# Four graph layers on one core: batches exchanged inside the row tiles, row mixing on 64x64 blocks, rows loaded four groups ahead

## The chip, the cores and the metric

The kernel runs on 1 core of one Trainium2 chip. Time is device time of one execution in microseconds (us); lower is better. A core has five instruction queues that run beside one another: TensorE (PE, matrix products; its weight loads are shown as PEld), VectorE (DVE), ScalarE (ACT), GpSimd (POOL) and SyncE (SP, which here only issues DMAs). All data are f32.

## The reference, cut to what matters

There are 128 batches of 64 nodes with 256 features, and one 64x64 matrix `adj` that all layers share. Four layers follow one another, each with a residual and a layer norm.

```python
w = adj * adj                                       # layer 0: three graph convolutions
h = relu(w @ (x @ W1)); h = relu(w @ (h @ W2))
x = layernorm(x + w @ (h @ W3))
# layer 1: U = eigenvectors of the normalized Laplacian of adj
x = layernorm(x + U @ (relu((U.T @ x) @ W1 + b1) @ W2 + b2))
# layer 2: two graph convolutions (Wg0, Wg1), then for p = 1..4 an LSTM over windows of p nodes;
#          its last hidden state replaces node p-1 of each window
x = layernorm(x + h)
# layer 3: attention among the 64 nodes of a batch, masked by adj
x = layernorm(x + softmax(mask(h @ h.T)) @ h + b)   # h = x @ W + b_lin
```

## The kernel before, in words

The 8192 rows (128 batches x 64 nodes) are cut into 16 groups of 8 batches. A group is a tile of 128 partitions, 4 columns of rows and 256 features: column t holds two batches, one in partitions 0 to 63 and one in 64 to 127. Four groups live in `X` and twelve in `XA`; `order` is the sequence in which layer 0 takes them (groups 4 to 15, then 0 to 3).

**Phase A** is `layer0`, one loop over the groups. `burst` (its matmuls are L1068) mixes by `w` and transposes in one step: 32 matmuls of 64x64 blocks, one for each of the four corners of the array in turn. The three weight products are done by Strassen's seven products each (`seven`, with `by_first`, `by_second`, `by_third`; their matmuls all have line L977). The last convolution's mixing is `mix_rows`: before the change two calls per group, each one matmul of the full 128x128 block-diagonal `sqT2` over 512 moving columns (also L977; in the profile `ps<-s,sqT`, two PE instructions for one f32 matmul), then a DVE addition to the rows and the pieces of the layer norm. `bank` hands out PSUM banks in turn: 3 with the tag `ps`, 2 `ch`, 2 `b5`. `step` holds back a product's PSUM reader until the next product is issued and pops one piece of a norm.

Beside the matmuls runs `eigen`, the eigenvectors of the Laplacian: a long chain of tiny DVE steps (L52 with the other DVE work of this phase, its PE steps L312). It is a generator that `between` advances by a counted clock `now`, so its instructions stand between those of the products at fixed places. PE, DVE, ACT and POOL run in the order of the program text here (`manual_schedule`). SP, and the ten lines after `layer0` (L1235 to L1244: row sums of `adj`, halved and summed biases, written as `rs_row`, `adH2`, `rs_col`, `wide["c_b0"]`, `cbi`, `dbb`), were outside of this and were put by a scheduler: it set five of those DVE instructions among the first 51 us.

All input DMAs but three go through SP, in this order: a group, `aw1`, `aw2`, a group, `aw3`, the other 14 groups (L921), the constants of `eigen` (L924), and then the weights and biases of later layers (L890 to L959). After them SP issues `sh<-sh` and `sh<-h` (L1174, L1175) for each group, copies that `by_third` needs, and `rest<-XA`, the finished rows of a group.

**Phase B** is layers 1 to 3, all with line L162: `unit` records the operations of two groups at a time in a `Plan`, which simulates them with written costs and emits them engine by engine, up to four units in flight. `left_over` is what was left of phase A's norm pieces. The last two groups (`ENDING`, 14 and 15) take a shorter way through `from_lstm` and `layer3`: transposes on PE, attention in two halves of a group, norms whose scaling is on ACT (`scalar=True`, with `nm`, the negative mean times `rs`). `long` is the LSTM for p = 3 and 4 on two groups at once, `fast` one step of it; the last step's result is written in the order node, batch.

## Time and profile before

| what | value |
|---|---|
| median of 3 runs | 2268.37 us (2267.16 to 2269.09) |
| the profiled execution's own time | 2269.74 us, span 2267.9 us, mean granted TensorE clock 0.995 |
| PE, DVE, ACT, POOL busy | 2222.0, 1758.5, 1241.2, 207.9 us |
| phase A, start to the last `mix_rows` | 0 to about 821 us |
| phase B | about 821 us to the end |
| DMA | 163.05 MB, 264 GB/s in the first 57 us, 72 GB/s in the mean |

The profile is one execution. "busy" is time in which an engine had an instruction; the idle time before an instruction is put down to what it waited for ("<-"). The timeline gives start and duration of merged runs of like instructions. For PE the starts are what to read: a duration contains the way through the array, and the next matmul starts before it is over. One f32 matmul is two PE instructions. The view by stretches gives, for each stretch of the span, its length and the busy time and number of instructions of PE, PEld, DVE, ACT and POOL, then the granted clock, the busy share of the DMA engines (as the view reckons it) and GB/s.

### The profile page before, as it was taken

The numbers are of one execution on the slowest core, as the hardware profiler recorded it, in microseconds if no ns is written. First come the engines' busy times: TensorE is split into PE (matmuls) and PEld (weight loads), VectorE is DVE, ScalarE is ACT, GpSimd is POOL, SyncE is SP. The second block draws the span as 40 slices with busy tenths as digits, with TensorE's granted clock in tenths as the row PEclk, the third lists the DMA queues.
The fourth block names the chain that finished last, engine by engine and source line by source line (L and its number), as shares of the span: only waits on it lengthen the run. The fifth ranks groups of instructions, "written<-read, shape, count | busy, mean of one in ns | idle before, by whom it ended". The sixth has DMA issues, their size and how long they took to land.

```text
span 2267.9 us, 53164 instructions
## 1 busy us (share of the span) xinstructions
PE 2222.0 (98%) x20840; PEld 2026.8 (89%) x20840; DVE 1758.5 (78%) x5925; ACT 1241.2 (55%) x2999; POOL 207.9 (9%) x390
## 2 busy tenths in 40 slices
PE   7999999999999999999999999999999999999996
PEld 5998888888888878999999999999999999999985
DVE  5888888878888759765967977977977877578977
ACT  3455555545554445665655655655655655566554
POOL 0111111111111110000100000000000010000112
PEclk9999999999999999999999999999999999999998
DMA  8443333344332240000211211211211211002331
GB/s 264 96 92 77 85 75 85 87 91 94 85 85 66 66 155 29 20 1 20 76 38 41 78 66 50 78 57 50 87 57 41 84 65 35 31 29 65 109 113 54
DMA packets 95243, 163.05 MB, mean 72 GB/s; under 512 B 24976, under 2 KB 65936, under 8 KB 94992
## 3 DMA queue, kind: packets, MB, share of 16 engines
q1 hardware_dynamic: 83840, 120.05, 15.8%
q0 software_dynamic: 10800, 39.33, 9.2%
q8 instruction: 164, 2.69, 0.5%
q14 instruction: 87, 0.71, 0.1%
q10 hardware_dynamic: 352, 0.28, 0.0%
HBM read 57.64 MB, written 45.09 MB: 45 GB/s over the span
## 4 chain that ended last, share of the span: by engine, by line
PE 89%; DVE 6%; DMA 2%; ACT 1%; issue 1%; SPq 1%; POOL 1%; ACTq 0%; POOLq 0%; DVEq 0%
PE ps L162 59%; PE ch L977 15%; PE b L977 7%; PE ps L977 6%; PE ps L1068 2%; DVE w L162 1%; PE pa L312 1%; DVE D L52 1%; DMA XA<-in_x_dram 1%; DVE gates L162 1%; DVE X L162 1%; ACT gates L162 0%; DVE h L52 0%; DVE tw L52 0%; SPq L921 0%
## 5 line engine op out<-in xcount | busy, mean ns | idle before, releaser
L162 PE MATMUL ps<-w,wih 128*128 128x128 f32 (+2 forms) x2944 | 572.8, 298 | 2.1 <-DVE gates L162 0.9
L162 PEld LDWEIGHTS ps<-w,wih 128*128 128x128 f32 x2944 | 453.8, 191 | 28.5 <-issue 6.2
L162 PE MATMUL ps<-w,sums 128*128 128x128 f32 (+2 forms) x3104 | 476.6, 293 | 0.0
L162 PEld LDWEIGHTS ps<-w,sums 128*128 128x128 f32 x3104 | 423.5, 191 | 14.1 <-issue 1.9
L162 ACT ACTIVATE gates<-gates,cbi 128x256 f32<-128x256 f32 (+4 forms) x736 | 314.0, 479 | 174.0 <-DVE gates L162 172.0
L162 DVE TENSOR_TENSOR gates<-gates,ps 128x512 f32<-128x512 f32 (+4 forms) x408 | 234.2, 585 | 173.1 <-PE ps L162 159.7
L162 ACT COPY gates<-ps 128x512 f32<-128x512 f32 (+4 forms) x408 | 203.8, 505 | 253.8 <-PE ps L162 247.8
L986 ACT ACTIVATE h<-h 128x512 f32<-128x512 f32 x141 | 88.8, 629 | 283.3 <-DVE h L52 283.2
L162 PE MATMUL ps<-hs,whh 128*128 128x128 f32 (+1 forms) x896 | 181.2, 284 | 0.1
L162 PE MATMUL ps<-w,whh 128*128 128x128 f32 (+1 forms) x896 | 181.1, 284 | 0.0
L162 POOL TENSOR_SCALAR rs<-mv 128x2 f32<-128x2 f32 x96 | 27.5, 297 | 1318.5 <-DVE mv L162 1317.0
L162 ACT ACTIVATE gates<-ps,cbi 128x128 f32<-128x128 f32 (+2 forms) x368 | 119.1, 383 | 43.4 <-PE ps L162 43.1
L162 PEld LDWEIGHTS ps<-hs,whh 128*128 128x128 f32 x896 | 139.7, 191 | 0.3 <-DVE hs L162 0.3
L162 PEld LDWEIGHTS ps<-w,whh 128*128 128x128 f32 x896 | 139.7, 191 | 0.0
L977 PE MATMUL ch<-m,tw 128*128 128x256 f32 x512 | 120.6, 380 | 3.5 <-DVE h L52 3.5
L977 PE MATMUL b<-ss,aw 128*128 128x256 f32 x512 | 122.6, 379 | 0.0
L977 PEld LDWEIGHTS ch<-m,tw 128*128 128x128 f32 x512 | 96.2, 190 | 17.2 <-DVE h L52 4.7
L977 PEld LDWEIGHTS b<-ss,aw 128*128 128x128 f32 x512 | 96.3, 190 | 12.7
L1060 POOL DMA_DIRECT2D sh<-h x60 | 53.2, 957 | 485.9 <-PE b L977 148.8
L162 ACT ACTIVATE gates<-c 128x256 f32<-128x256 f32 (+1 forms) x176 | 75.5, 433 | 27.9 <-DVE c L162 26.2
L162 PE MATMUL ps<-hs,sums 128*128 128x128 f32 (+1 forms) x448 | 90.6, 284 | 0.0
L162 DVE TENSOR_TENSOR w<-w,w 128x128 f32<-128x128 f32 (+2 forms) x264 | 80.5, 316 | 8.9 <-PE ps L162 4.4
(384 smaller groups left out, 4281.2 us busy)
## 6 DMA issues: line engine op xcount, KB each, us to landing
sh<-h POOLq DMA_DIRECT2D x60, 512.0 KB, 5.8
far<-w SPq DMA_DIRECT2D x42, 512.0 KB, 2.8
w<-far SPq DMA_DIRECT2D x168, 128.0 KB, 3.1
X<-rest SPq DMA_DIRECT2D x24, 512.0 KB, 3.4
out_dram<-X SPq DMA_DIRECT2D x64, 128.0 KB, 1.8
sh<-sh SPq DMA_DIRECT2D x15, 512.0 KB, 2.9
sh<-h SPq DMA_DIRECT2D x15, 512.0 KB, 2.9
sh<-sh POOLq DMA_DIRECT2D x15, 512.0 KB, 4.6
```

The costliest lines, as they stand in the source:

```text
L52: return getattr(self.engine, name)(out, *args, **kw)
L162: getattr(e, name)(*[real(x) for x in args], **{k: real(v) for k, v in kw.items()})
L312: PE.matmul(out, lhsT, rhs, start=True, stop=True)
L977: PE.matmul(out, lhsT, rhs, start=start, stop=stop, **kw)
L986: S.activation(dst, src, AF.Relu)
L1060: nc.gpsimd.dma_start(out, src, accum_op=ALU.add)
L1068: PE.matmul(p[h][m, k, t, :], src[hs, t, f], sqT2[hs, hs], start=True, stop=True)
```

## The change

1. Column 2u+j of a group now holds in its half h the batch 4(2g+u)+2h+j; before, h and j were exchanged (4(2g+u)+2j+h). So loads and stores of rows (`fetch`, `found`) are DMAs of 64 partitions x 2 columns instead of 128 partitions (1 or 2 columns), four for each group; `burst` of the rows lands in batch order in `m1`; and `mix_rows` is one call per group with eight matmuls of 64x64 blocks over 256 moving columns, in two PSUM banks, followed by two DVE additions.
2. `AHEAD = 4`: the first four groups are loaded at the start, the others one group per turn of `layer0`, four groups ahead. The constants, small weights and biases go to a list `later`, of which each turn issues two. SP is now in `manual_schedule` in phase A.
3. The ten lines after `layer0` become `small_things`, called in the turn n-4 (the 13th of 16).
4. Last two groups: before the last LSTM step (p = 4, t = 3) the state `hT` is copied to batch order (`turned`), and the step writes its result there; `from_lstm` loses its eight copies. In `norm(scalar=True)` three POOL instructions become two DVE ones.

```diff
...
-    def given(g):
-        return x_t[:, 4 * g:4 * g + 4, :]
+    def fetch(queue, g, u):
+        for h, hs in enumerate(halves):
+            queue.dma_start(rows_of(g)[hs, 2 * u:2 * u + 2, :], given[2 * g + u, h])
...
     nc.sync.dma_start(adst[N:, :], adj)
-    nc.scalar.dma_start(rows_of(order[0])[:, 2:4, :], given(order[0])[:, 2:4, :])
-    for t in range(2):
-        nc.sync.dma_start(rows_of(order[0])[:, t, :], given(order[0])[:, t, :])
+    fetch(nc.scalar, order[0], 1)
+    fetch(nc.sync, order[0], 0)
     aw1 = load(wa, "aw1", a_w1, "(k p) f -> p k f", [P, 2, 512], p=P)
...
         nc.sync.dma_start(aw2[:, :, cols], a_w2.rearrange("(k p) f -> p k f", p=P)[:, :, cols])
-    for g in order[1:]:
-        for t in (0, 2):
-            nc.sync.dma_start(rows_of(g)[:, t:t + 2, :], given(g)[:, t:t + 2, :])
+    for g in order[1:AHEAD]:
+        for u in range(2):
+            fetch(nc.sync, g, u)
         if g == order[1]:
             aw3 = load(wa, "aw3", a_w3, "(k p) f -> p k f", [P, 8, D], p=P)
-    nc.sync.dma_start(eig_c, consts)
+    later = [(eig_c, consts)]
+    def load(pool, name, src, pattern, shape, **kw):
+        t = pool.tile(shape, F32, name=name)
+        later.append((t, src.rearrange(pattern, **kw)))
+        return t
...
     cb1 = keep.tile([P, 2], F32, name="cb1")
-    nc.sync.dma_start(cb1, c_b1)
+    later.append((cb1, c_b1))
     wide = {}
     for name, src in (("b_b1", b_b1), ("b_b2", b_b2), ("c_b0", c_b0), ("d_b", d_b)):
         wide[name] = keep.tile([P, src.shape[0]], F32, name=f"wide_{name}")
-        nc.sync.dma_start(wide[name], src.partition_broadcast(P))
+        later.append((wide[name], src.partition_broadcast(P)))
     cbi = keep.tile([P, 4, 8], F32, name="cbi")
     cbh = keep.tile([P, 4, 8], F32, name="cbh")
-    nc.sync.dma_start(cbi, c_bi)
-    nc.sync.dma_start(cbh, c_bh)
+    later.append((cbi, c_bi))
+    later.append((cbh, c_bh))
...
     def burst(dst, src, c):
-        to = dst.rearrange("p c (t h n) -> p h c t n", h=2, n=N)
-        p = [bank().rearrange("p (c t n) -> p c t n", c=2, t=4) for _ in range(2)]
+        n = N if src is h1 else P
+        to = dst.rearrange("p c (t h n) -> p h c t n", h=2, n=n)
+        b = [bank() for _ in range(2)]
+        p = [x.rearrange("p (c t n) -> p c t n", c=2, t=4) for x in b]
...
             for h in range(2):
-                S.copy(to[:, h, c:c + 2], p[h])
+                S.copy(to[:, h, c:c + 2], b[h].rearrange("p (c t n) -> p c t n", c=2, n=n))
...
-    def mix_rows(g, t):
-        p = bank().rearrange("p (t f) -> p t f", t=2)
-        mm(p, sqT2, s3[:, t:t + 2, :])
+    def mix_rows(g):
+        p = [bank().rearrange("p (u f) -> p u f", u=2) for _ in range(2)]
+        for u in range(2):
+            for j, js in enumerate(halves):
+                for h, hs in enumerate(halves):
+                    PE.matmul(p[h][js, u, :], sqT2[hs, hs], s3[hs, 2 * u + j, :], start=True, stop=True)
+        now[0] += QUADS
+        between()
         def result():
-            x2 = rows_of(order[g])[:, t:t + 2, :]
-            VL.tensor_add(x2, p, x2)
-            norms.extend(scalar_norm(tc, small, x2, half, spare))
-            if t and order[g] >= RING:
-                norms.append(lambda: nc.sync.dma_start(rest[order[g]], rows_of(order[g])))
+            rows = rows_of(order[g])
+            for h in range(2):
+                VL.tensor_add(rows[:, h::2, :], p[h], rows[:, h::2, :])
+                norms.extend(scalar_norm(tc, small, rows[:, h::2, :], half, spare))
+            if order[g] >= RING:
+                norms.append(lambda: nc.sync.dma_start(rest[order[g]], rows))
...
+    def small_things():
+        pr = bank()
+        PE.matmul(pr[:, :P], ones, adT2, start=True, stop=True)
+        V.tensor_copy(rs_row, pr[:, :P])
+        V.tensor_scalar(adH2, adT2, 0.5, None, op0=ALU.mult)
+        V.tensor_reduce(rs_col, adst, AX.X, ALU.add)
+        V.tensor_scalar(wide["c_b0"], wide["c_b0"], rs_col, None, op0=ALU.mult)
+        V.tensor_add(cbi, cbi, cbh)
+        V.tensor_add(dbb, dbb, dbl)
+        for q in (slice(0, 4), slice(6, 8)):
+            V.tensor_scalar(cbi[:, :, q], cbi[:, :, q], 0.5, None, op0=ALU.mult)
...
             last = g == n - 1
+            if g + AHEAD < n:
+                for u in range(2):
+                    fetch(nc.sync, order[g + AHEAD], u)
+            for to, of in later[2 * g:2 * g + 2]:
+                nc.sync.dma_start(to, of)
...
                     next(some, None)
+            if g == n - 4:
+                small_things()
             if last:
-                for t in (0, 2):
-                    mix_rows(g - 1, t)
+                mix_rows(g - 1)
                 for _ in plain():
                     pass
-                for t in (0, 2):
-                    mix_rows(g, t)
+                step()
+                mix_rows(g)
...
             if g:
-                mix_rows(g - 1, 0)
+                mix_rows(g - 1)
             next(w1)
...
             VL.tensor_sub(X12, X12, sx[:, 1])
-            if g:
-                mix_rows(g - 1, 2)
...
     with tc.manual_schedule(engines={mybir.EngineType.PE, mybir.EngineType.DVE, mybir.EngineType.Activation,
-                                     mybir.EngineType.Pool}):
+                                     mybir.EngineType.Pool, mybir.EngineType.SP}):
...
-    pr = bank()
-    PE.matmul(pr[:, :P], ones, adT2, start=True, stop=True)
-    V.tensor_copy(rs_row, pr[:, :P])
-    V.tensor_scalar(adH2, adT2, 0.5, None, op0=ALU.mult)
-    V.tensor_reduce(rs_col, adst, AX.X, ALU.add)
-    V.tensor_scalar(wide["c_b0"], wide["c_b0"], rs_col, None, op0=ALU.mult)
-    V.tensor_add(cbi, cbi, cbh)
-    V.tensor_add(dbb, dbb, dbl)
-    for q in (slice(0, 4), slice(6, 8)):
-        V.tensor_scalar(cbi[:, :, q], cbi[:, :, q], 0.5, None, op0=ALU.mult)
...
             V.bn_aggr(mv[:, t, :], st[:, t, :])
-        if twice:
+        if scalar:
+            V.tensor_scalar(rs, mv[:, :, 1], eps, None, op0=ALU.add)
+        elif twice:
             G.tensor_scalar(rs, mv[:, :, 1], eps, 0.25, op0=ALU.add, op1=ALU.mult)
...
             nm = plan.tile("nm", [P, 2])
-            G.tensor_scalar(nm, mv[:, :, 0], -1.0, None, op0=ALU.mult)
-            G.tensor_tensor(nm, nm, rs, ALU.mult)
+            V.scalar_tensor_tensor(nm, mv[:, :, 0], -1.0, rs, op0=ALU.mult, op1=ALU.mult)
...
         if g in ENDING:
-            hb = as3(work(), 2)
-            for bs in (slice(0, 4), slice(4, 8)):
-                for k, copy, cost in ((0, V.tensor_copy, 0.33), (1, S.copy, 0.56)):
-                    copy(as3(hb[:, k, :], 8)[:, bs, :], hT[:, k, :, bs].rearrange("p n b -> p b n"), cost=cost)
+            hb = hT.rearrange("p k b n -> p k (b n)")
...
             norm(x2, ending)
-            at = 4 * g + first + t
-            for j in range(2):
-                Q.dma_start(out_t[:, at + j, :], x2[:, j, :])
+            for h, hs in enumerate(halves):
+                Q.dma_start(found[2 * g + (first + t) // 2, h], x2[hs])
...
             for w in range(2):
-                turn_out(seen(h, w, p - 1), o[:, w], t[:, w])
-        c, hs = state("c", 8 * nw), None
+                turn_out(turned[w][:, h, :, p - 1::p].rearrange("p b n -> p n b") if new is None and turned
+                         else seen(h, w, p - 1), o[:, w], t[:, w])
+        c, hs, turned = state("c", 8 * nw), None, []
         for t in range(p):
             x = [[seen(k, w, t) for w in range(2)] for k in range(2)]
             new = state("hs", 8 * nw) if t < p - 1 else None
+            if ending and new is None:
+                for hT in hTs:
+                    turned.append(work().rearrange("p (k b n) -> p k b n", k=2, b=8))
+                    for k, copy in ((0, V.tensor_copy), (1, S.copy)):
+                        copy(turned[-1][:, k], hT[:, k].rearrange("p n b -> p b n"), cost=0.8 if k else 0.6)
             fast(p, 8 * nw, x, hs, c, new, write)
...
             hs = new
+        hTs[:] = turned or hTs
...
                     if g == RING - 1 - i // 14:
-                        half = np.arange(4 * D) // (2 * D) == i // 7 % 2
+                        half = np.arange(4 * D) // D % 2 != i // 7 % 2
...
         for p in (3, 4):
-            long(hTs, p)
+            long(hTs, p, p == 4 and groups[0] in ENDING)
         late = plan.late
...
```

More of the change, by code (lines that the diff above doesn't have):

```diff
@@ L778 @@
 RING = 4
+AHEAD = 4
 QUADS = 1.17
@@ L869 @@
     NT = ROWS // P
-    x_t = x.rearrange("b n f -> (b n) f").rearrange("(t p) f -> p t f", p=P)
-    out_t = out.rearrange("b n f -> (b n) f").rearrange("(t p) f -> p t f", p=P)
+    given, found = (v.rearrange("(q h j) n f -> q h n j f", h=2, j=2) for v in (x, out))
+    halves = slice(0, N), slice(N, P)
     uid = [0]
@@ L1257, with load @@
     psb = ctx.enter_context(tc.tile_pool(name="psb", bufs=1, space=bass.MemoryType.PSUM, reuse_waits="tile"))
+    def load(pool, name, src, pattern, shape, **kw):
+        t = pool.tile(shape, F32, name=name)
+        nc.sync.dma_start(t, src.rearrange(pattern, **kw))
+        return t
     wih, whh = [], []
@@ L1762, in pairs, with long @@
         fast(2, 128, x[1], hs=hs, c=c, write=write)
-    def long(hTs, p):
+    def long(hTs, p, ending):
         nw = 64 // p
```

## The prediction

> **What bounds the kernel now.** First the page's busy times, then the view by stretches (stretch, its length, busy time of PE, PEld, DVE, ACT, POOL, granted clock, DMA share, GB/s):
>
> ```profile
> PE 2222.0 (98%) x20840; PEld 2026.8 (89%) x20840; DVE 1758.5 (78%) x5925; ACT 1241.2 (55%) x2999; POOL 207.9 (9%) x390
> ...
> 0.00:60.00 60.00, 45.91 (x416) 33.72 (x417) 34.41 (x141) 18.28 (x39) 2.96 (x11) 1.00 0.84 260
> 60.00:460.00 400.00, 398.91 (x3694) 356.61 (x3692) 329.53 (x1659) 205.85 (x532) 52.73 (x84) 1.00 0.37 86
> 460.00:800.00 340.00, 337.28 (x3067) 296.32 (x3066) 279.15 (x1085) 167.94 (x387) 43.22 (x73) 1.00 0.34 78
> ...
> 822.00:900.00 78.00, 69.83 (x1049) 62.23 (x1050) 71.61 (x175) 42.83 (x102) 9.55 (x21) 0.96 0.27 106
> 900.00:2200.00 1300.00, 1297.26 (x12135) 1217.36 (x12134) 993.80 (x2714) 765.34 (x1844) 82.81 (x156) 1.00 0.17 56
> ...
> 2226.00:2268.00 42.00, 26.65 (x176) 20.43 (x176) 28.56 (x102) 21.01 (x50) 12.19 (x36) 0.83 0.12 39
> ```
>
> PE is the bound nearly everywhere. It idles 14.1 us in the first 60, 3.8 in 60 to 800, 8.2 in 822 to 900, 2.7 in 900 to 2200 and 15.4 in the last 42. So there are two ways to gain: less PE work, or shorter idle time at the two ends and at the change of phase.
>
> Next the waits of DVE and of PE in the first 60 us (total, times, longest):
>
> ```profile
> DVE dbb L1242 <- DMA dbb<-in_d_b_dram: 5.2, 1, 5.2
> ...
> DVE wide_c_b L1240 <- DMA wide_c_b<-in_c_b_dram: 2.7, 1, 2.7
> ```
>
> ```profile
> PE ch L977 <- DVE h L52: 3.0, 2, 2.4
> PE pa L312 <- DVE LV L52: 2.1, 1, 2.1
> PE ch L977 <- issue: 1.6, 1, 1.6
> ```
>
> DVE stands from 39.31 to 44.48 for a 1 KB bias that no product needs before layer 3, and again up to 48.24; what PE needs is queued behind. PE therefore stands 2.07 us up to 45.69, 0.51 up to 49.24 and 2.44 up to 53.68.
>
> Third, PE's timeline, for the price of the mixing (starts count):
>
> ```profile
> 704.54 1.02 PE L977 MATMUL ps<-s,sqT 128*128 128x512 f32 x2
> 705.40 1.03 PE L977 MATMUL ch<-aw,m 128*128 128x256 f32 x4
> 706.26 1.95 PE L977 MATMUL ps<-aw,h 128*128 128x128 f32 x16
> ...
> 721.31 2.05 PE L977 MATMUL b<-tv,sh 128*128 128x128 f32 x16
> 723.29 1.16 PE L1068 MATMUL ps<-sqT,h 64*64 64x64 f32 x64
> 724.39 2.05 PE L977 MATMUL ch<-tv,h 128*128 128x128 f32 x16
> ```
>
> Last, the chain near the end:
>
> ```profile
> 2227.46 0.66 ACT w L162
> 2228.17 5.18 PE ps L162 x15
> ...
> 2240.16 1.54 POOL rs L162 x3
> 2241.76 0.66 POOL nm L162 x3
> ...
> 2263.54 0.22 POOL nm L162
> ```
>
> **The change part by part**, against the profiled execution (2269.74 us).
>
> *Row mixing, −7.7.* Removed: two products of 705.40−704.54 = 0.86 us a group, 1.72. Added: eight block products, 16 PE instructions of 256 columns, 4096 columns in all, as many as a burst's 64 instructions of 64. The pair of a 16-instruction product and a burst takes 724.39−721.31 = 3.08; the product alone takes 1.79 (702.75 to 704.54), which leaves 1.29 for the burst. Moving 64 columns takes 0.86×64/(2×512) = 0.054 us an instruction, so 64 in single file would take 3.4: the trace shows four corners running side by side, 16 rounds in 0.86, and 0.43 for entering and leaving. For the new step I take the same 1.29, less 0.05 for fewer instructions: 1.24. Gain 0.48 × 16 = 7.7. From below, no cost of entering: 0.86, −13.8. From above, nothing side by side: 3.44+0.4 = 3.84, +33.9; only pairs: 1.72+0.4, +6.4. The burst is the nearest row: same corners, same rotation, same columns. The two PSUM banks are now taken at once, and the next use of the bank comes some 3.9 us later; DVE's addition began 0.6 to 2.3 us after such a product, so I count no stall. If that cover goes it costs up to 0.15 a group, 2.4.
>
> The trace's own 0.43 us speaks here: 128x128 work gives way to 64x64 blocks and back. [...]
>
> *Early stall, −5.0.* The steps on `dbb`, `wide["c_b0"]` and `cbi` leave the first 51 us and run in turn 13 (near 640 us), when the biases have landed long before; SP issues two small loads a turn. DVE's 7.9 us of standing and the 5.0 us of PE idle behind them go. What comes next: the third wait was partly DVE's backlog of `eigen` steps, which stays but is 7.9 us earlier. Bounds: −6.0 (other idle goes too) and 0 (`ch` waits as long for something else).
>
> *PE's wait on "issue", 1.6 us from 25.45, −0.8.* It falls in 20 to 40 us, where DMA moves 346 GB/s. In front now stand four groups and the products' weights, about 6.4 MB, so loading is dense until about 21 us instead of 41. Whether the wait comes from the load the trace doesn't say: half, bounds −1.6 and 0.
>
> *Start, +0.4.* The first rows come as 64-partition DMAs. The first burst begins at 5.02, after `adH` (whose 0.22 us on DVE go: −0.1). The whole-partition transfers of this kernel move 346 GB/s, so 512 KB take 1.5 us; at half that rate it would be 3.0. The present rows, issued at 1.3 and 1.4, land 3.2 to 3.3 later, by 4.7, which leaves 0.3 before the burst; and both halves are under way together, so I stay near the lower end. Bounds 0 and +1.5; the other groups' rows are never what PE waits for. Four loads instead of two a group cost SP about one more us a group, where it is idle after 45 us.
>
> [...]
>
> *`small_things`, +0.3.* One PE product (0.22) and about 1.75 us of DVE (0.16 to 0.35 each, by the rows in 39 to 51 us) stand in one block in turn 13. DVE is 82% busy there (279.15 of 340), so 1.4 us of slack come within some 10 us. Bounds 0.2 and 2.0.
>
> *Change of phase, −0.5 with `adH`.* The product for `rs_row` (0.22) and the 0.50 us before it go; against them both halves' additions to the rows (0.69 each) come after one step. I take −0.4. The clock is granted at half for some us twice in 822 to 900, and moved work may meet that: bounds −2 and +2.
>
> *Ending, −2.5.* Eight copies go (four on ACT at 0.59, four on DVE); the copies to batch order go before the last step, beside PE's work. PE waits 3.1 us at 2227.3 behind the present ones. From 2229.1 the row addition could begin 1.1 earlier. Of each norm, POOL's `rs` (0.22 to 0.30) and two `nm` (0.22+0.20) become two DVE steps: about 0.5 less on the chain, in two norms, 1.0. The power (0.71) stays on POOL, and DVE's `nm` now waits for it: behind it on DVE stands the other half's `st` and `mx`, about 1 us, which the next norm waits for. The last stores now need both columns: +0.4. So −1.1 −1.0 −0.8 (shorter wait at 2227.3) +0.4 = −2.5; bounds −5 and +1.
>
> *The plan of phase B, 0.* Its matmuls are the same in number and PE is idle 2.7 of 1300 us; other emission may cost or give 2.4, as much as its longest wait (2.4, for a transfer near 2174).
>
> Sum: −7.7 −5.0 −0.8 +0.4 −0.1 +0.3 −0.4 −2.5 = −15.8, 2253.9 for the profiled execution. That one lies 1.4 over the median of the runs (2268.37), so 2252.5.
>
> **The rivals.**
> - *Blocks don't run side by side* (slower). Place: `mix_rows`. Price in single file +33.9 for −7.7: about 2294. For: no row has 256-column blocks. Against: the burst. The rest of the change is worth −8.1, so the kernel is slower by over 4.5 us from 1.72+(8.1+4.5)/16 = 2.5 us a group. At pairs (2.1) it is 2267, no change.
> - *Another wait takes the stall's place*: the 5.0 are not gained, 2257.5. For: `eigen` is a serial chain, and its DVE steps fill DVE to 11.5 of each 20 us. Against: DVE stood waiting for a DMA when PE starved.
> - *The ending or the plan gives nothing or costs*: DVE's `nm` holds the other half, or the replanned order loses 1 to 2: 2256 to 2259.
> - *Entering blocks is free and the early idle goes wholly*: −6.1 −1.0, about 2245.5.
> - *The freed PE time is not used in phase A*, since DVE, 82% busy, becomes late: half the mixing gain, 2256.5.
>
> **How the numbers follow.** A measurement of this kernel tells about 0.2%, 4.5 us, from no change: under 2263.8 is faster. Chances: forecast, 2249 to 2256, 0.50; early wait replaced 0.14; ending or plan 0.13; DVE late 0.06; better, 2244 to 2248, 0.07; pairs or several prices together, 2264 to 2272, 0.04; single file 0.06. Faster 0.90, same 0.04, slower 0.06. The range 2245 to 2262 leaves out the last two and some of the better case.
>
> **What would show it.** From a block step's start to the next product 1.24 us (2.5 would make me wrong); no DVE wait for `dbb` or `wide_c_b`, and PE idle about 8 instead of 14.1 in the first 60 us; the last `mix_rows` near 807 instead of 821; from 2226's last LSTM step to the end 2 to 3 us less. Wrong if PE's idle in 60 to 800 rises over 10 us.

## The result, and the profile after

| | kernel before | changed kernel |
|---|---|---|
| median, runs | 2269.2 us, 9 runs (2267.16 to 2271.78) | 2264.06 us, 9 runs (2260.98 to 2266.58) |
| the profiled execution's span | 2267.9 us | 2262.4 us |

The ratio is 0.9974, with a 95% interval of 0.9964 to 0.9984. The kernel is faster by 5.1 us, where 15.9 were forecast; the time lies above the upper end of the range, 2262.

The page's busy times of the changed kernel, and its stretches in the same cuts as before (stretch, its length, busy time of PE, PEld, DVE, ACT, POOL, granted clock, DMA share, GB/s):

```profile
PE 2217.8 (98%) x21032; PEld 2025.6 (90%) x21032; DVE 1756.1 (78%) x5939; ACT 1242.2 (55%) x2997; POOL 198.4 (9%) x366
...
0.00:60.00 60.00, 51.41 (x444) 39.23 (x444) 37.78 (x154) 20.47 (x45) 4.70 (x13) 0.97 0.59 158
60.00:460.00 400.00, 397.99 (x3804) 357.48 (x3803) 327.02 (x1644) 207.79 (x535) 51.80 (x84) 1.00 0.43 100
460.00:800.00 340.00, 336.23 (x3142) 295.97 (x3142) 279.38 (x1091) 168.24 (x383) 42.55 (x72) 1.00 0.34 81
...
822.00:900.00 78.00, 69.76 (x929) 61.40 (x928) 69.71 (x172) 43.54 (x101) 7.97 (x18) 0.98 0.18 66
900.00:2200.00 1300.00, 1299.33 (x12150) 1217.56 (x12148) 992.50 (x2713) 765.65 (x1841) 79.04 (x156) 1.00 0.18 56
```

PE is idle 8.6 instead of 14.1 us in the first 60, as forecast. But from 60 to 800 it is idle 5.8 us instead of 3.8, and the 78 us after the change of phase are no fuller than before, though they now begin 8 us later in the work.

The waits of PE in the first 60 us (total, times, longest):

```profile
PE ps L1076 <- DMA XA<-in_x_dram: 2.0, 2, 1.3
PE ps L1076 <- ACT h L992: 1.7, 2, 1.6
PE ps L983 <- ACT m L1082: 1.0, 2, 0.7
```

The waits for DVE's `h` and `LV` and the one on "issue" are gone. Two waits for the first rows are new.

PE's timeline at a block step (starts count):

```profile
695.96 1.95 PE L983 MATMUL ch<-aw,h 128*128 128x128 f32 x16
697.84 1.09 PE L1149 MATMUL ps<-s,sqT 64*64 64x256 f32 x16
698.87 1.13 PE L983 MATMUL ch<-aw,m 128*128 128x256 f32 x4
699.83 0.38 PE L983 MATMUL ps<-aw,h 128*128 128x128 f32 x2
```

The step takes 1.03 us from its start to the next product. The product ahead of it takes 1.88 instead of 1.79, and the one behind it 0.96 instead of 0.86, so the price is 1.22; forecast were 1.24.

To see where the time went, the same piece of work is followed through the traces: the first burst on `h1` at the end of a turn, in us from the start (turn 0: the first one, before the loop), the start of the last mixing instruction, and the span.

| kernel | turn 0 | 1 | 2 | 12 | 13 | 15 | last mixing | span |
|---|---|---|---|---|---|---|---|---|
| before | 20.1 | 73.0 | 122.6 | 622.9 | 671.2 | 771.1 | 820.9 | 2267.9 |
| changed | 21.4 | 69.7 | 119.8 | 614.0 | 664.5 | 763.3 | 812.9 | 2262.4 |
| difference | +1.4 | -3.3 | -2.8 | -8.9 | -6.8 | -7.8 | -8.0 | -5.5 |

Three things stand out. Between turns 2 and 12 the kernel gains 0.6 us a turn, where 0.48 were forecast for the mixing. Turn 1 gains 4.7 us, less than the 5.8 of the stall and the wait on "issue"; turn 2 loses 0.5 and turn 13 loses 2.1. And 2.5 of the 8.0 us gained by the last mixing are gone at the end of the span. The experiments take these in turn.

One thing in these traces has nothing to do with the change: the clock granted to PE. It was at half for 3.4 us from 22.2 us on in the changed kernel's profiled execution, and at full there in others with the same instructions. The stretches from 20 to 25 us of the changed kernel, of pool_norm (which differs from it only in the last two groups) and of fetch_mid, both described below:

```profile
20.00:25.00 5.00, 2.79 (x90) 2.47 (x94) 0.90 (x8) 2.90 (x7) 0.00 (x0) 0.72 0.63 162
```

```profile
20.00:25.00 5.00, 2.23 (x107) 1.84 (x110) 1.56 (x8) 2.90 (x7) 0.00 (x0) 1.00 0.83 180
```

```profile
20.00:25.00 5.00, 2.51 (x128) 2.23 (x128) 1.17 (x8) 2.90 (x7) 0.00 (x0) 1.00 0.58 139
```

Turn 1 takes 48.2 to 48.3 us in the changed kernel, whole_mix and spread, where such a stretch falls into it, and 47.2 in pool_norm, copies_back and whole_stores, where none does. So this stretch costs 1.1 us, and a comparison of turn 1 holds only at the same clock.

### The profile page after: what moved, and what is told of

Its sections match the earlier page's. It is cut to its first block, busy times and chain, and to the rows that moved or that the text cites. A ratio compares the mean times of both kernels' runs of the same rounds, so it can differ in the third digit from the quotient of the medians.

```text
span 2262.4 us, 53587 instructions
## 1 busy us (share of the span) xinstructions
PE 2217.8 (98%) x21032; PEld 2025.6 (90%) x21032; DVE 1756.1 (78%) x5939; ACT 1242.2 (55%) x2997; POOL 198.4 (9%) x366
## 2 busy tenths in 40 slices
DMA packets 95740, 163.07 MB, mean 72 GB/s; under 512 B 25472, under 2 KB 66432, under 8 KB 95488
## 4 chain that ended last, share of the span: by engine, by line
PE 86%; DVE 8%; DMA 2%; ACT 2%; issue 1%; SPq 0%; POOL 0%; DVEq 0%; ACTq 0%; POOLq 0%
PE ps L162 57%; PE ch L983 15%; PE b L983 7%; PE ps L983 4%; PE ps L1076 2%; DMA sh<-h 1%; DVE w L162 1%; DVE X L162 1%; PE pa L312 1%; DVE D L52 1%; DVE gates L162 1%; DVE h L52 1%; DVE tw L52 1%; PE ps L1149 1%; ACT gates L162 1%
## 5 line engine op out<-in xcount | busy, mean ns | idle before, releaser
L162 PEld LDWEIGHTS ps<-w,sums 128*128 128x128 f32 x3104 | 423.6, 191 | 15.7 <-ACT gates L162 2.5
L162 ACT ACTIVATE gates<-ps,cbi 128x128 f32<-128x128 f32 (+2 forms) x368 | 119.8, 385 | 44.3 <-PE ps L162 44.0
L162 POOL TENSOR_SCALAR rs<-mv 128x2 f32<-128x2 f32 x88 | 22.4, 265 | 1292.9 <-DVE mv L162 1292.1
L983 PE MATMUL b<-ss,aw 128*128 128x256 f32 x512 | 122.6, 379 | 0.0
L162 DVE SCALAR_TENSOR_TENSOR c<-gates,c 128x256 f32<-128x256 f32 (+1 forms) x112 | 49.8, 445 | 44.6 <-ACT gates L162 44.5
```

The source lines that it names most:

```text
L162: getattr(e, name)(*[real(x) for x in args], **{k: real(v) for k, v in kw.items()})
L983: PE.matmul(out, lhsT, rhs, start=start, stop=stop, **kw)
```

## The experiments

All but pad64 were measured side by side with the kernel before, whose median was 2268.7 to 2269.5 us there. The intervals of the ratios are about 0.1% to each side, some 2 to 3 us. What is smaller is read from the traces, one execution of each kernel.

### The mixing with the whole array again (whole_mix)

```diff
-        for u in range(2):
-            for j, js in enumerate(halves):
-                for h, hs in enumerate(halves):
-                    PE.matmul(p[h][js, u, :], sqT2[hs, hs], s3[hs, 2 * u + j, :], start=True, stop=True)
+        for h in range(2):
+            PE.matmul(p[h], sqT2, s3[:, 2 * h:2 * h + 2, :], start=True, stop=True)
```

> The changed kernel, but each group's row mixing is two products of the full 128x128 matrix over 512 columns again, in the same place and the same two PSUM banks (rows come out mixed from the wrong batches, the work is otherwise the same). Theory 1, the block step is worth its price difference on the path: 1.72 instead of 1.22 us on PE for each of 16 groups, so +8.0 us over the changed kernel, about 2272. Rival, the PE time that the blocks free in phase A is lost again to waits for other engines: +0 to +2 us, 2264 to 2266. Phase A (start to the last mixing) ends 8 us later by the first, 0 to 2 later by the second.

Measured: 2267.1 us (ratio to before 0.9989, 0.9981 to 0.9998), 3.0 more than the changed kernel. The last mixing starts at 819.9, 7.0 later; between turns 2 and 12 the difference is 5.1 us, 0.51 a turn. Of the 7.0 us, 0.6 are there already at turn 0, and turn 13 takes as long in both kernels (50.4 and 50.5 us). So the first theory holds in phase A, nearly to the size. But the advantage of the blocks falls to 5.2 us by 870 us, and the spans differ by 3.0. What is lost up to 870 is the matter of the experiments with tiny products below: with whole-array mixing there is no wait of PE on "issue" between 815 and 905 us, in the changed kernel there are 3.5 us of it. The rest goes after 890 us, where kernels with the same ending differ by up to 2.6 us from one profiled execution to another (see the ending below).

### The small steps alone (before_late)

```diff
+    def small_things():   # the ten lines that stood after layer0, unchanged
...
+            if g == n - 4:
+                small_things()
             if last:
```

> The kernel before, with one part of the change alone: the ten lines on biases and row sums are called in turn 13 instead of standing after the loop (loads, row layout, mixing and ending as before). Theory: PE's 5.0 us of idle time between 43 and 54 us go, and the block costs 2.4 us in turn 13 as it does in the changed kernel (48.3 us for that turn before, 50.4 after, where the cheaper mixing alone would make 47.8), so -2.6 us against the kernel before, and PE idle near 9 instead of 14.1 in the first 60 us. Rival 1, another wait takes the place of the early one: PE idle there stays over 12 and the kernel is 1 to 3 us slower than before. Rival 2, the block is free by itself and dear only beside the new mixing, whose two PSUM banks it competes with: -5 us.

Measured: 2266.15 us (ratio 0.9985, 0.9977 to 0.9994), 2.9 less than before. The stall went: the end of turn 1 is at 68.5 instead of 73.0, 4.6 of it after turn 0. Turn 13 took 49.1 us, 0.8 more than before, so the block costs 0.8 there, and not the 2.4 expected. So the early term was right; and the block's high price belongs to the combination with the new mixing (rival 2 in part). The total agrees with the first theory only by accident: of the 3.6 us that were left at the last mixing, 0.8 were lost afterwards.

### The small steps spread (spread)

```diff
-            if g == n - 4:
-                small_things()
+            if n // 2 <= g < n - 4:
+                for _ in range(2):
+                    norms.append(small_things.pop(0))   # now a list of eight steps
```

> The changed kernel, but the small steps of turn 13 are spread two a turn over turns 9 to 12, each at a place where a piece of a norm would be done. Theory: as one block they hold DVE for 2 us, the additions that free the two PSUM banks of the mixing come late and PE waits: that turn takes 2.4 us too much; spread they cost 0.3 in all, so -2 us against the changed kernel. Rival: the cost lies in the steps themselves on a nearly full DVE and only moves to other turns: within 0.5 us.

Measured: 2260.95 us (ratio 0.9965, 0.9952 to 0.9977), 3.1 less than the changed kernel. In the traces it is 2.4: turn 13 takes 47.8 us instead of 50.4, which is the 48.3 of before less the 0.5 of the mixing, so the block cost 2.6 us there; and turns 9 to 12, which now hold the steps, take 0.2 more in all. PE's timeline in the changed kernel shows how:

```profile
649.63 2.33 PE L983 MATMUL ps<-aw,h 128*128 128x128 f32 x16
653.03 1.13 PE L983 MATMUL ps<-aw,m 128*128 128x256 f32 x4 [1.06 <-DVE XA L52]
```

and DVE's timeline in the same kernel:

```profile
645.97 0.29 DVE L1173 COPY rs_row<-ps 128x128 f32<-128x128 f32 x1 [2.05 <-PE ps L1172]
...
652.29 1.29 DVE L52 TENSOR_TENSOR XA<-ps,XA 128x512 f32<-128x512 f32 x2
```

With the steps spread, the same two products on PE:

```profile
650.65 1.95 PE L983 MATMUL ps<-aw,h 128*128 128x128 f32 x16
652.44 1.03 PE L983 MATMUL ps<-aw,m 128*128 128x256 f32 x4
```

The mixing began at 647.6 and holds two of the three `ps` banks. They come free by the two additions on DVE. These stand behind the block of small steps and the `eigen` steps, and begin only at 652.3, 4.7 us after the mixing. `ps<-aw,m` needs a bank, and PE waits. In the kernel with whole-array mixing in one step, which also takes two banks at once, turn 13 takes 50.5 us; in the kernel before, which takes one bank at a time, the same block costs 0.8.

### The row loads in the middle of the turn (fetch_mid)

```diff
-            if g + AHEAD < n:
-                for u in range(2):
-                    fetch(nc.sync, order[g + AHEAD], u)
-            for to, of in later[2 * g:2 * g + 2]:
-                nc.sync.dma_start(to, of)
+            def loads():   # the same lines
...
-                (0, 5): lambda: (less(2, 1, 0), nc.sync.dma_start(sh[:, 1], sh[:, 2])),
+                (0, 5): lambda: (less(2, 1, 0), nc.sync.dma_start(sh[:, 1], sh[:, 2]), loads()),
```

> The changed kernel, but a turn's four row loads and two small loads are issued right after the copy sh<-sh, some 10 us before the copy sh<-h, instead of at the start of the next turn, which on the queue is right after the copy sh<-h. Theory: the row loads lie beside the accumulating copies sh<-h (1.5 to 3 us more between these than before, PE waits of 0.22 and 0.73 us on them in turns 1 and 2, and what follows from them): these waits go, -1.5 to -2.5 us against the changed kernel. Rival: the copies are late for another reason (GpSimd, ACT), and the time stays within 0.5 us; or the loads now delay sh<-sh and it is slower.

Measured: 2261.76 us (ratio 0.9965, 0.9952 to 0.9979), 2.3 less than the changed kernel. In the traces it is 2.2 less already at the end of turn 2, where it stays; but 1.1 of these are the clock. From turn 0 the changed kernel needs 31.4 us to the products of `aw` by `h` at 52.8 us, and this one 30.2, just as pool_norm, copies_back and whole_stores do at the same clock with the loads unmoved. From there to the end of turn 1 it is 16.9 us against 15.7, and turn 2 takes 50.1 against 49.9. So the loads cost about 1.4 us, a little less than the theory's least. The queue SP in the changed kernel, and GpSimd's accumulating copies of the same turn:

```profile
98.35 0.52 SPq L1206 DMA_DIRECT2D sh<-h  x1
98.92 3.61 SPq L907 DMA_DIRECT2D XA<-in_x_dram  x4
```

```profile
98.68 0.89 POOL L1066 DMA_DIRECT2D sh<-h  x1 [33.41 <-PE ch L983]
104.09 0.87 POOL L1066 DMA_DIRECT2D sh<-h  x1 [4.53 <-DMA sh<-h]
```

The same copies in the kernel with the loads moved:

```profile
96.69 0.89 POOL L1066 DMA_DIRECT2D sh<-h  x1 [35.28 <-PE ch L983]
100.55 0.87 POOL L1066 DMA_DIRECT2D sh<-h  x1 [2.98 <-DMA sh<-h]
```

The rows are asked for at the start of a turn in the program, but on the queue this is right behind the last copy of the turn before. The two copies and half a megabyte of rows are then under way together; the copies' chain is 1.55 us longer, and PE waits for it in `by_third`, 0.22 us in turn 1 and 0.73 in turn 2:

```profile
111.43 2.05 PE L983 MATMUL b<-tv,sh 128*128 128x128 f32 x16 [0.73 <-DMA sh<-h]
```

PE never waits for these rows, but it does for what they delay.

### Stores by whole columns (whole_stores), and four edits at once (best1)

```diff
-            for h, hs in enumerate(halves):
-                Q.dma_start(found[2 * g + (first + t) // 2, h], x2[hs])
+            for j in range(2):
+                Q.dma_start(found[2 * g + (first + t) // 2, :, :, j], x2[:, j, :])
```

> The changed kernel, but layer 3 stores one column over all 128 partitions with each DMA (its two halves go to two batches) instead of two columns over 64 partitions. Theory: the last stores go at 205 GB/s in the changed kernel and at 290 before, and from the last ACT instruction to the end it takes 4.45 us instead of 2.74; with whole columns this gap is under 3 us and the kernel 1 to 1.7 us faster than the changed one. Rival: the gap comes from four stores ready at once, since the last two norms end together; then it stays over 4 us and the time within 0.5 us.

> The changed kernel with four edits at once: row loads issued in the middle of the turn (-2.3 us alone), the small steps spread over turns 9 to 12 (-3.1 alone), whole columns for the stores (expected -1 to -1.7), and the first group's rows loaded as four whole columns. Theory: the first three are at different places and add up, and the first rows come some 0.5 us earlier: 2264 - 2.3 - 3.1 - 1.3 - 0.5 = 2257. Rival: half of what is gained in phase A is lost again at the change of phase, 2260.

Measured: 2312.83 us (ratio 1.0188) and 2320.91 us (1.0228). Theories and rivals alike missed, by about 49 us and by 61 to 64. SP's timeline of the first:

```profile
2250.08 53.29 SPq L162 DMA_DIRECT2D out_dram<-X  x16
```

These stores move 48 GB/s. The destination of such a DMA has two batches as its outermost dimension. The last eight stores of the changed kernel leave 128 packets of under 512 B beside their rows, 16 each. The whole trace of whole_stores holds 24576 such packets, that of the changed kernel 25472; the difference is 14 for each of the 64 stores, which leaves two each. While the last stores run, the mean busy share of the 16 DMA engines is one to two tenths, where it is seven to nine tenths under the last stores of the changed kernel. From both, an estimate: such a store runs on 2 of the 16 engines. In best1 the first rows, loaded in this way, kept PE waiting for 14.3 us. So, of the two ways to move the exchanged batches that ran, halves are the faster (about 200 GB/s in the changed kernel), and these two kernels tell nothing of what halves cost.

### Whole, contiguous partitions at both ends (whole_wrong)

```diff
-    fetch(nc.scalar, order[0], 1)
-    fetch(nc.sync, order[0], 0)
+    nc.scalar.dma_start(rows_of(order[0])[:, 2:4, :], x_t[:, 2:4, :])
+    for t in range(2):
+        nc.sync.dma_start(rows_of(order[0])[:, t, :], x_t[:, t, :])
...
-            for h, hs in enumerate(halves):
-                Q.dma_start(found[2 * g + (first + t) // 2, h], x2[hs])
+            for j in range(2):
+                Q.dma_start(out_t[:, at + j, :], x2[:, j, :])
```

> The changed kernel with the first group's rows loaded and all rows of layer 3 stored in whole partitions that are contiguous, as before the change (these rows then belong to other batches than the reference's; the work is the same). Theory: transfers of 64 partitions are slower one by one: the last stores 205 instead of 290 GB/s, a packet of 1 KB 73 instead of 46 ns; from the last ACT instruction to the end 4.45 becomes under 3 us, and the first two steps on the rows no longer wait for DMA (2.0 to 3.2 us in the runs of the changed layout, in two waits). Together -2 to -2.5 us against the changed kernel. Rival: the first rows are late because of what else is loaded and the last because two norms end at once: within 0.7 us.

Measured: 2261.17 us (ratio 0.9963, 0.995 to 0.9975), 2.9 less than the changed kernel. The last two scalings on ACT begin at 2255.88 in the changed kernel and at 2254.71 here; the spans are 2262.4 and 2259.6. So 1.6 of the 2.8 us come after that point, from the stores alone. The other 1.2 are there by the last mixing, and the half clock of the changed kernel's turn 1, which this execution did not have, makes 1.1 of them. The rates in the last 15 us, changed kernel first (one slice is 0.38 us):

```profile
GB/s 0 0 0 0 0 0 0 0 0 0 0 0 0 0 0 85 210 200 191 191 194 210 139 0 0 0 0 128 202 205 180 194 208 205 77 0 0 0 0 0
```

```profile
GB/s 0 0 0 0 0 0 0 0 0 0 0 0 0 0 0 0 0 3 303 254 227 276 309 27 0 0 22 0 0 52 292 287 246 243 279 0 0 0 0 0
```

Halves go at about 200 GB/s, whole partitions at about 270. The first rows, though, gain nothing: the first burst on `h1` is at 21.6 us, as late as in the other kernels with the changed loads (20.9 to 22.3, against 20.1 before), and one of the two waits for rows is replaced by one of 1.9 us for `aw`. What makes the first 20 us slower by about 1.4 us stands on DVE. The sums of weights begin there with `tw<-aw`, in the kernel before, the changed kernel and this one:

```profile
13.89 1.21 DVE L52 TENSOR_TENSOR tw<-aw 128x1024 f32<-128x1024 f32 x1
```

```profile
15.23 1.22 DVE L52 TENSOR_TENSOR tw<-aw 128x1024 f32<-128x1024 f32 x1 [0.74 <-DMA aw<-in_a_w_dram]
```

```profile
15.45 1.23 DVE L52 TENSOR_TENSOR tw<-aw 128x1024 f32<-128x1024 f32 x1 [0.70 <-DMA aw<-in_a_w_dram]
```

In all three the burst on `h1` follows 6.2 us later. So the delay is in part the later first rows (0.5 us in the changed kernel) and in part the weights `aw`, for which DVE did not wait before. From 12 to 20 us all loads together move about 350 GB/s before and 250 to 270 in the other two. Whether the halves of the other groups' rows make the difference, no run separates.

The two halves are issued one right after the other here, and the rate measured at the end, about 200 GB/s, is about 0.7 of that of whole partitions.

### The two halves of the new ending (pool_norm, copies_back)

```diff
-        if scalar:
-            V.tensor_scalar(rs, mv[:, :, 1], eps, None, op0=ALU.add)
-        elif twice:
+        if twice:
...
-            V.scalar_tensor_tensor(nm, mv[:, :, 0], -1.0, rs, op0=ALU.mult, op1=ALU.mult)
+            G.tensor_scalar(nm, mv[:, :, 0], -1.0, None, op0=ALU.mult)
+            G.tensor_tensor(nm, nm, rs, ALU.mult)
```

> The changed kernel, but the norms of the last two groups take 1/sqrt and the scaled mean on GpSimd as before (rs and nm not on DVE). Theory of the prediction: two norms on the last chain get 0.5 us longer, +1.0 us. Rival, read from the trace since: in the last 16 us DVE runs without a break, so what it is spared (0.15 us for each of four steps in the last window) comes back on the same chain: -0.3 to +0.5 us.

Measured: 2264.12 us (ratio 0.9975, 0.9966 to 0.9984), no difference from the changed kernel. Its trace is another matter. Its halves end one after the other again, as before the change:

```profile
2259.85 1.09 ACT L162 ACTIVATE X<-X,nm,rs 128x256 f32<-128x256 f32 x2 [3.81 <-POOL nm L162]
```

and from 890 us (the mark explained below) to the end it takes 2.8 us longer than the changed kernel's. That execution was 2.8 us slower than the median of its kernel, so this trace does not settle what the norms give.

```diff
-            hb = hT.rearrange("p k b n -> p k (b n)")
+            hb = as3(work(), 2)   # and the four copies a group, as before
...
-            long(hTs, p, p == 4 and groups[0] in ENDING)
+            long(hTs, p, False)
```

> The changed kernel, but the last LSTM step writes in the order node, batch and the last two groups are copied to batch order after it, in four copies a group, as before the change. Theory of the prediction: PE waits 1.3 us longer after the last LSTM product, and the first row addition comes 1.1 us later: +1.9 us. Rival: the last 12 us are set by DVE and the stores, with both halves ready at once, and PE's gain before is lost there: within 0.5 us, or a gain if the halves come one after the other again.

Measured: 2263.58 us (ratio 0.9976, 0.9966 to 0.9985), no difference again, to within some 2 us. PE does wait longer after the last LSTM product (3.2 us instead of 1.8), and the trace from 890 us to the end is 1.3 us longer than the changed kernel's; the medians show neither. In the changed kernel ACT's timeline ends

```profile
2255.88 2.07 ACT L162 ACTIVATE X<-X,nm,rs 128x256 f32<-128x256 f32 x4 [2.34 <-DVE nm L162]
```

with four scalings in one go, where the kernel before ends with two:

```profile
2264.07 1.09 ACT L162 ACTIVATE X<-X,nm,rs 128x256 f32<-128x256 f32 x2 [2.87 <-POOL nm L162]
```

Both halves of the last group now end together: from the start of PE's last product to the last scaling 5.6 us pass instead of 4.7, the scalings take 1.0 us more, and the four stores behind them 1.7 more. PE's last product comes 9.1 us earlier than before the change, the end only 5.5.

How much the whole ending gives can be read over more kernels. The products of `X` by `adH` near 890 us are the mark, before the change and after:

```profile
896.49 1.16 PE L162 MATMUL ps<-adH,X 64*64 64x64 f32 x64
```

```profile
890.28 1.16 PE L162 MATMUL ps<-adH,X 64*64 64x64 f32 x64
```

From there to the end the kernel before takes 1371.4 us, and before_late, with the same ending, 1371.3. The changed kernel takes 1372.1. It and the seven kernels that have its ending and its stores (whole_mix, spread, fetch_mid, pad, pad64, best2, best3) take 1369.9 to 1372.5, in the mean 1371.4. So behind this mark the change gains nothing in the mean.

### Tiny products at the start (pad, pad64, best3)

```diff
...
+        for _ in range(16):
+            PE.matmul(pd[:N, :8], ones[:N, :N], ones[:N, :8], start=True, stop=True)
         PE.transpose(pt[:N, :P], adst, ident)
+        for _ in range(16):   # pad64: 32 and 32; best3: 8, 6 and 6 in idle places
+            PE.matmul(pd[:N, :8], ones[:N, :N], ones[:N, :8], start=True, stop=True)
```

> The changed kernel with 32 tiny products more (64x64 by 8 columns, 128 PE instructions with their weight loads; results unused) in the first 5 us, where PE waits for the first rows. Theory: PE's waits of 1.8 and 1.7 us on 'issue' at 817 and 825 us come from its instructions being fetched (16 KB at 816.8 and 824.1) right behind the dense bursts while 5 MB of weights are loaded; where they fall is set by the number of PE instructions before, 12 more a group than before and none of these waits in the kernel before or with whole-array mixing. 128 instructions move the fetches by half a block of 16 KB: the waits at the phase change move or change size by over 1 us in sum, and the time goes with them. Rival: they belong to the phase change itself (two waits of 1.8 and 1.7 at the same instructions, time within 0.5 us).

> The changed kernel with 64 tiny products more at the start, 256 PE instructions: one whole 16 KB block. Theory: the ends of the blocks fall on the same instructions as in the changed kernel, so the waits on 'issue' at the change of phase are back, 3 to 4 us in two waits at the same two places (the fifth product of w by bw, the fourth of v by bw); the start is some 5 us later. Rival: the 32 tiny products took the waits away in another way (a warmer clock, later loads), and with 64 there are still none.

PE's timeline at the change of phase, changed kernel:

```profile
816.71 0.70 PE L162 MATMUL ps<-bw,w 128*128 128x128 f32 x4
819.21 3.29 PE L162 MATMUL ps<-bw,w 128*128 128x128 f32 x28 [1.80 <-issue]
...
823.98 0.92 PE L162 MATMUL ps<-bw,v 128*128 128x256 f32 x3
826.63 1.35 PE L162 MATMUL ps<-bw,v 128*128 128x256 f32 x5 [1.73 <-issue]
```

The same with 32 tiny products (pad):

```profile
820.01 3.83 PE L162 MATMUL ps<-bw,w 128*128 128x128 f32 x32
...
826.14 1.99 PE L162 MATMUL ps<-bw,v 128*128 128x256 f32 x8
```

And with 64 (pad64):

```profile
823.35 0.70 PE L162 MATMUL ps<-bw,w 128*128 128x128 f32 x4
826.47 4.90 PE L162 MATMUL ps<-bw,w 128*128 128x128 f32 x28 [2.42 <-issue]
...
832.85 1.99 PE L162 MATMUL ps<-bw,v 128*128 128x256 f32 x8
```

The trace of the changed kernel holds instruction packets of 16 KB, 165 on one queue (q8) for 42064 instructions of PE and PEld: about 255 instructions to a packet. Two of them, of 0.9 and 1.1 us, are at 816.8 and 824.2 us, just where the waits are. With 128 PE instructions more, half a packet, both waits are gone; with 256 more, a whole packet, the larger one is back at the very same instruction, 2.42 us instead of 1.80. The second is not: there PE waits for something else (2.7 us for DVE a little later). So the place of these waits goes with the number of PE instructions before them. The block mixing has 24 more a group, weight loads counted, 384 and so one and a half packets in all, and without these (whole_mix) there is no such wait. The waits cost less than their length: whole_mix waits 2.6 us for DVE instead and is granted 0.66 of the clock from 835 to 840 us, and the blocks' advantage shrinks by 1.8 us, not by 3.5. That they are so long because 5 MB of weights are loaded at that time (410 GB/s) was not tried.

Pad as a whole was measured at 2262.69 us (ratio 0.9967, 0.9955 to 0.998). It is 3.9 us late at the last mixing, through its own 1.6 us and a longer wait for `sh<-h` (2.25 us, with 3.4 us at half clock behind it: 0.84 and 0.82 granted in the 5 us from 60 and from 65), and level with the changed kernel 11 us later. Pad64 was run once: 2272.95 us, with the tiny products on the path.

### The two edits that paid, together (best2, best3)

> The changed kernel with the row loads issued in the middle of the turn and the small steps spread over turns 9 to 12, and nothing else. Theory: the two add up, 2264.1 - 2.3 - 3.1 = 2258.7. Rival: they share a cause or lose the gain at the change of phase: about 2260.5.

Best2 is spread and fetch_mid in one kernel. Measured: 2258.24 us (ratio to before 0.9952, 0.994 to 0.9965), where 2258.7 were expected. The two add up. At the last mixing its trace is 4.9 us ahead of the changed kernel's: 2.4 by the steps, 1.4 by the loads and 1.1 by the clock. This is the fastest of all kernels here (best3 below is level), 11 us faster than the kernel before and 5.8 faster than the changed one.

> The kernel with mid-turn loads and spread small steps (2258.2 us, PE waiting 3.8 us on 'issue' between 808 and 905 us) with 20 tiny products more, 80 PE instructions, placed where PE is idle in the first 22 us. Theory: the waits belong to where the blocks of PE's instructions end; 80 of 256 instructions earlier is about half way to what 128 did (none left, -3.7 us from the last mixing to 30 us after it), so 1 to 3.8 us less waiting on 'issue' there, and with up to 1.5 us for the tiny products themselves 2255 to 2258. Rival: the waits stay over 3 us, time 2258.5 to 2260.

Best3 adds 20 tiny products to best2. Measured: 2258.73 us (ratio 0.9951, 0.9937 to 0.9964). The waits on "issue" at the two places are gone, and 30 us into phase B nothing is left of it: PE is 2.3 us ahead of best2 at one point and 1.3 behind soon after, for it now waits 2.6 us for DVE, is granted 0.66 of the clock from 825 to 830 us, and meets another wait on "issue" of 1.6 us. The waits moved; the time is that of best2. So the theory on their place holds and the expected gain doesn't.

## Why the prediction was wrong

| step | predicted | measured | by |
|---|---|---|---|
| start, with `adH2` | +0.3 | +1.4 | turn 0 in the two traces |
| early stall, wait on "issue" | -5.8 | -5.8 (-6.9 at full clock) | turn 0 to 55 us |
| row loads | 0 | +1.4 | fetch_mid, at the same clock |
| row mixing | -7.7 | -6.9 | whole_mix, turn 0 to the last mixing, and the 0.5 of turn 13 |
| `small_things` | +0.3 | +2.6 | spread, turn 13 |
| change of phase, to 900 us | -0.4 | +1.8 | the two traces |
| phase B to the last LSTM products | 0 | +1.0 | the two traces |
| ending | -2.5 | -0.3 | the two traces |

The measured column sums to -4.8 against -5.5 in the traces. What is missing are in part small waits that no row holds: between turns 2 and 12 whole_mix, too, is 1.0 us faster than the kernel before.

**What was right.** The two large terms. The burst was the right row for the block step (1.22 us for 1.24), and the rival that blocks don't run side by side is out. The early stall was what it seemed, and no other wait took its place (4.6 us by before_late alone, which had half clock for part of turn 1).

**Where it failed.** Not in one step, but in all the small terms to one side.

*"Start, +0.4."* The term asked when the first rows land and nothing else. They cost 0.5 us; 0.8 more came from the weights `aw`, which land later beside the new loads and for which DVE now waits. That its upper bound, +1.5, lies near the measured 1.4 is luck: with whole first rows the delay is the same (whole_wrong). The bound took rows at half the rate, an estimate that no run shows: at the end halves moved about 200 GB/s and whole partitions about 270. About 5.9 MB were in front, not 6.4.

*"`small_things`, +0.3."* The bounds 0.2 and 2.0 counted the steps and DVE's slack. The cost came from what the steps delay, the two bank-freeing additions. The prediction had named this cover, "DVE's addition began 0.6 to 2.3 us after such a product, so I count no stall", and had not asked what happens in the turn in which DVE gets nearly two more microseconds in front of that addition.

*"The other groups' rows are never what PE waits for."* True, and beside the point: the transfers that PE does wait for run at the same time, and this cost 1.4 us. The step left out the place on SP's queue to which the loads were moved.

*"Change of phase, -0.4."* The 192 more PE instructions (16 for 4, in each group), and as many weight loads, were priced by the prediction in PE time alone. That they also move the points at which instructions are fetched was not thought of: 3.5 us of waits on "issue", and +1.8 us by 900 us instead of -0.4. The prediction had even met such a wait (1.6 us at 25.45 us) and had put half of it down to the loads.

*"Ending, -2.5."* The sum was -1.1 -1.0 -0.8 +0.4. It came to nothing. The stores cost 1.6, not 0.4 (whole_wrong). What the copies and the norms on DVE gave, the medians of copies_back and pool_norm don't show, and their traces, 1.3 and 2.8 us longer, don't settle it. PE's own gain was there, 3.9 us from the last LSTM products on, but the last 12 us aren't PE's: the chain that ends last is DVE's, with two norms at once, and then the stores'. The sum has no term for two norms that end together.

**The rivals.** None of them was the case. Nearest was "the ending or the plan gives nothing", at 2256 to 2259; what happened was that together with costs in four other places that no rival names. The direction was right, though narrowly: the gain is 0.23%, and the prediction's own limit for "faster" was 0.2%. The range was too narrow, since it treated the small terms as if they erred to both sides.

## What to carry to other kernels

When work is moved to a busy engine, price not the moved instructions but what stands behind them: here 1.8 us of steps on an 82% busy DVE cost 2.6 us on PE, because two banks were freed behind them, and the same steps spread over four turns cost 0.2. When loads are moved later, look where they land on the queue, and which transfers of the loop are under way then (1.4 us here). Before a difference between two traces is put down to an edit, compare the granted clock in that stretch (3.4 us at half cost 1.1 us here). And of a gain in PE time near the end, see what is left behind another engine's chain: here PE's last product came 9.1 us earlier, and the end 5.5.

## What was not expected of the hardware

- A DMA between 128 partitions and two separate batches in memory left two packets of under 512 B instead of 16 (the count of whole_stores against the changed kernel's) and moved 48 GB/s, against about 270 for whole contiguous partitions and 200 for halves.
- PE waited 1.80 and 1.73 us at the change of phase of the changed kernel, where instruction packets of 16 KB were fetched (816.8 and 824.2 us). The place went with the count of PE's instructions before: 165 such packets stand beside 42064 instructions, 128 more took both waits away, and 256 more brought one of the two back to the same instruction, with 2.42 us.
- The clock was granted at half (0.50) for 3.4 us at a time, twice in the first 2200 us of the changed kernel's profiled execution, from 22.2 and from 868.7 us, and for 10.2 us from 2223.8. The place is not always the same: the 5 us from 20 and from 25 have 0.72 and 0.94 there, and 1.00 in pool_norm, copies_back and whole_stores, whose first 60 us are the same instructions. This stretch cost 1.1 us. Such stretches are likely part of the scatter between the runs: of the nine of the changed kernel, the one with a mean granted clock of 0.997 took 2260.98 us, and the three with 0.994 took 2264.23 to 2266.58.
